# A two-layer attention and feed-forward kernel: three changes where the first feed-forward meets the second attention

## The chip, the cores and the metric

The kernel runs on one core of a Trainium2 chip. The metric is device time in microseconds (us) of one launch, as the median of several runs. Lower is better.

The engines are named as the profile names them: PE is TensorE (PEld its weight loads), DVE is VectorE, ACT is ScalarE, POOL is GpSimd, SP is SyncE, which here only issues DMAs.

## The reference

Two layers, each an attention and a feed-forward, work on `x` of 2 x 1024 tokens by 512. Every part is normed before and after and added to the stream.

```python
x = x + ln(L0_attn(ln(x)))      # per-token attention over groups of heads, no mixing of tokens
x = x + ln(L0_ffn(ln(x)))       # weights rounded to -1, 0, 1; hidden size 1408
x = x + ln(L1_attn(ln(x)))
x = x + ln(L1_ffn(ln(x)))       # silu(gate) * up, 2 of 4 kept; hidden size 2048

def L1_attn(x):                 # 16 heads of 32, 4 key and value heads, causal
    q, k, v = rope(x @ q_w.T), rope(x @ k_w.T), x @ v_w.T
    logits = einsum('bhqd,bhkd->bhqk', q, repeat(k, 4)) / sqrt(32)
    probs = softmax(logits + causal_mask)
    return einsum('bhqk,bhkd->bhqd', probs, repeat(v, 4)) @ c_w.T
```

The change touches the end of `L0_ffn` and all of `L1_attn`.

## The kernel before, in words

**Tiles and groups.** The 2048 tokens are 16 tiles of 128; four tiles make a group of 512 (`GT` = 4, `NG` = 4). `x` stays in SBUF as `x_sb`.

**First feed-forward.** For each group `g` a loop runs over 11 chunks `hc` of the hidden size. A chunk is 16 products into two PSUM banks (`l0_hidden`, L381), a sigmoid on ACT, a product on DVE (L387), a cast on ACT (L389) and a difference on POOL (L390), and later 8 products into four banks `po` (`l0_out`, L400) that stay open for the whole group. The output products trail the chunks through the list `pend`; at chunk 2 none are issued, and the last ones of a group fall into the first two chunks of the next. After the last, DVE and ACT norm the four banks and POOL adds them to `x_sb` (L421).

**The next stage's parts.** During the chunks of the last group the kernel already projects the tiles of batch 0 for the second attention. `project_parts` returns three functions per tile: `first` norms the tile and transposes it (`pxt`, `xT`), `second` makes `pq` and `pkv` (L570, L575) and the rotary products on DVE, whose sums go to POOL (`ra`, L602), and `third` transposes the result (`pkT`, `pqT`), splits it into a high and a low half on ACT and DVE (L617, L618) and writes both halves to DRAM (`dq`, L622, on SP). In the loop they are placed at L809 to L828:

```python
if 1 <= hc <= 2 * GT:
    if hc % 2:
        parts[hc // 2][0]()
        if hc > 1:
            parts[hc // 2 - 1][2]()
    else:
        parts[hc // 2 - 1][1]()
elif hc == 2 * GT + 1:
    parts[GT - 1][2]()
```

After the fourth tile's `third`, at chunk 9, `fill_k` and `fill_q` read keys and queries back from `dq` (L650, L645) into the tile `qk`. At chunk 10 the first scores are interleaved with the last outputs.

**Attention in two passes.** There are 16 tasks: batch, query group `Q`, key head. A first pass makes the scores (`score_step`: `psc`, L665 and the mask L671), takes their maximum on DVE (`mxs`, L676) and sums their exponentials on ACT (L678). The exponentials themselves are thrown away: they go to a tile `junk` in SBUF, and only the sum (`sms`) is used. For task 0 the tile is borrowed from the feed-forward's `h`. From maximum and sum DVE forms one shift per row (`shifts`). A second pass makes the scores again, transposed and shifted (`prob_step`: `pst`, L970 and L977), and ACT's exponential (L983) writes probabilities `pT`; on diagonal blocks POOL zeroes what lies ahead (`affine_select`, L985). `value_step` multiplies by the values one step later (`po`, L999).

**Outputs.** When the four heads of a query group are done, `output_parts` gives one part per tile, run one per step: four products into a bank `py` (L1015), statistics, an inverse root in 13 small DVE instructions (`inverse_root`, L198 to L205), the norm from PSUM into `tmpy` (L209), and an addition to `x_sb` on POOL (L1023), held back by `soon` until the selects of the next step are issued.

**Order.** PE and POOL run in the order in which the program is written; in the stretches that the change touches, DVE, ACT and SP instructions are ordered by the framework's scheduler. The dictionary `due` says which parts run behind which of the 96 steps of the second pass. PSUM has 8 banks: four `a`, three `o`, one `v`; `ring` hands out the `a` and `o` banks in turn.

**Weight pieces.** Sums of the second feed-forward's weights are prepared on POOL (L473) in tiles of 8 blocks of which 7 are used.

Of the kernel before, what the change touches and what calls it, by code (L numbers as in the profile page):

```python
# [9 lines left out]
F32 = mybir.dt.float32  # L10
# [14 lines left out]
def two_layer_sandwich(  # L25
# [406 lines left out]

    def left_piece(pool, tag, bufs, n, i):

        w = pool.tile([P, 8, 2, P], F32, tag=tag, name=f"wl_{n}_{i}", bufs=bufs)
        nc.sync.dma_start(
            out=w[:, 0:4].rearrange("p b c m -> p (b c m)"), in_=(f1_wg, f1_wu)[i][n]
        )
        kept[n, i] = dw.tile([P, 4, 2, P], F32, tag="kept", name=f"kept_{n}_{i}")
        a11, a12, a22, a21, s1_, s2_, s4_ = (w[:, k] for k in range(7))  # L440
        return kept[n, i], w, (
            (s1_, a21, a22, ALU.add), (s2_, s1_, a11, ALU.subtract),
            (a21, a11, a21, ALU.subtract), (s4_, a12, s2_, ALU.subtract),
        )

    def right_piece(pool, tag, bufs, S, j):

        w = pool.tile([P, 8, HW], F32, tag=tag, name=f"wr_{S}_{j}", bufs=bufs)
# [207 lines left out]
    def score_step(tk, q, k, ii, ch, heads, bank, waste):  # L656


        g, i = tk.g, GT * tk.Q + ii
        k0 = ch * GW  # L660
        k1 = min(k0 + GW, (i + 1) * P)
        w = k1 - k0
        for r in heads:
            pa = bank(f"psc_{tk.nm}_{ii}_{ch}_{r}")
            nc.tensor.matmul(  # L665
                pa[:, :w], q.bitcast(F32R)[:, r, ii * P : (ii + 1) * P],
                k.bitcast(F32R)[:, g, :w],
                start=True, stop=True,
            )
# [6 lines left out]
            nc.vector.tensor_reduce(mx, pa[:, :w], AX.X, ALU.max, negate=True)  # L676
            junk = waste(f"junk_{tk.nm}_{ii}_{ch}_{r}")
            nc.scalar.activation(  # L678
                junk[:, :w], pa[:, :w], AF.Exp, bias=mx, accum_out=tk.sm[:, ii, r, ch : ch + 1]
            )  # L680

    with tc.manual_schedule(engines={mybir.EngineType.PE, mybir.EngineType.Pool}):
# [69 lines left out]
        for g in range(NG):  # L752
            nxt = None
            for hc in range(HC):
# [5 lines left out]
                    for c in range(DC):  # L760
                        quant_apply(w3, raw3, th3, c)
                if g == NG - 1 and hc == HC - 1:
                    def waste0(name):
                        return s0.tile([P, GW], F32, tag="h", name=name).bitcast(BF16)

                    tk = tasks[0]
                    score_sums(tk, aw)
                    halves = [
                        lambda ii=ii, r=r: score_step(
                            tk, tk.q, tk.st.k[0], ii, 0, range(r, r + 2), ps_a, waste0  # L770
                        )
                        for ii in range(GT) for r in (0, 2)
                    ]
# [17 lines left out]
                if g + 1 < NG:  # L791
                    if hc == 2:
                        at = l0_softmax(g + 1)
                        ao = l0_values(g + 1, at)
                    if hc == 3:
                        l0_add(g + 1, ao)
                    if hc == 4:
                        nxt = l0_xT_stats(g + 1)
                    if hc in (6, 7):
                        for k in (0, 1):  # L800
                            l0_xT_norm(nxt, 2 * (hc - 6) + k)
                    if hc in (7, 8):
                        ks = (2 * (hc - 7), 2 * (hc - 7) + 1)
                        l0_xT(nxt, ks, [ps_a(f"pt_f{g + 1}_{k}") for k in ks])
                else:

                    if hc == 0:
                        parts = [project_parts(batch(0), i, on_act=i > GT + 1) for i in range(TB)]
                    if 1 <= hc <= 2 * GT:  # L809
                        if hc % 2:  # L810
                            parts[hc // 2][0]()
                            if hc > 1:
                                parts[hc // 2 - 1][2]()
                        else:
                            parts[hc // 2 - 1][1]()
                    elif hc == 2 * GT + 1:
                        parts[GT - 1][2]()
                        done[0] = GT
                        parts[GT][0]()


                        tk = tasks[0]
                        tk.st = batch(0)
                        both = big("qk", F32)[:, : 2 * NKV * GW].rearrange(
                            "p (n r t) -> p n r t", n=2, r=REP
                        )
# [53 lines left out]
    def in_pieces(m, name):  # L880

        nonlocal n_pm
        pm = pms[n_pm % 2]
        n_pm += 1
        r1 = s1.tile([P, GT, REP], F32, tag="r1", name=f"r1_{name}")
        nc.vector.tensor_copy(pm[:, :, :, 0], m)
        nc.vector.tensor_tensor(r1, m, pm[:, :, :, 0], ALU.subtract)
        nc.vector.tensor_copy(pm[:, :, :, 1], r1)
        nc.vector.tensor_tensor(pm[:, :, :, 2], r1, pm[:, :, :, 1], ALU.subtract)
        return pm  # L890
# [52 lines left out]
    def shifts(tk):  # L943

        m, sm = tk.mx[:, :, :, 0], tk.sm[:, :, :, 0]
        if tk.Q > 0:
            n = tk.Q + 1
            m = s1.tile([P, GT, REP], F32, tag="mfin", name=f"mfin_{tk.nm}")
            nc.vector.tensor_reduce(m, tk.mx[:, :, :, :n], AX.X, ALU.min)
            d = s1.tile([P, GT, REP, n], F32, tag="md", name=f"md_{tk.nm}")  # L950
# [57 lines left out]

    def output_parts(st, Q):

        def part(ii):
            nm = f"{st.b}_{Q}_{ii}"
            py = ring(f"py_{nm}")
            for c in range(DC):
                nc.tensor.matmul(  # L1015
                    py, st.oT[Q][:, c, ii * P : (ii + 1) * P], wc1[:, c, :],
                    start=(c == 0), stop=(c == DC - 1),
                )
            mv, rs = ln_stats(s1, [py], f"y_{nm}", roots=False)
            xt = x_sb[:, st.b * TB + GT * Q + ii, :]  # L1020
            tmp = s1.tile([P, D], F32, tag="xn", name=f"tmpy_{nm}", bufs=1)
            ln_apply(tmp, py, mv, rs, 0)
            soon(lambda: nc.gpsimd.tensor_tensor(xt, xt, tmp, ALU.add))  # L1023

        return [lambda ii=ii: part(ii) for ii in range(GT)]

    tw = aw_stack.enter_context(tc.tile_pool(name="tw", bufs=1, side="right"))

# [53 lines left out]
    with tc.manual_schedule(engines={mybir.EngineType.PE, mybir.EngineType.Pool}):  # L1082
# [9 lines left out]
            s_end[tk.n] = n  # L1092
        pos = s_end[0]

        def waste(name):
            return s1.tile([P, GW], BF16, tag="junk", name=name, bufs=3)

        def scored(tk):
            shifts(tk)
            later(first[tk.n] - 1, [lambda: maxima_T(tk)])  # L1100
# [1 line left out]
        def scores_up_to(n, step, between=lambda: None):  # L1102
            nonlocal pos
            while pos < min(n, len(s_steps)):
# [3 lines left out]
                    assert loaded[0] > tk.n  # L1108
                    score_sums(tk, s1)
                for r in (0, 2):  # L1110
                    score_step(tk, tk.q, tk.st.k[ch], ii, ch, range(r, r + 2), ring, waste)
                    if r == 0:
                        between()
                pos += 1
# [544 lines left out]
```

## Time and profile before

| | us |
|---|---|
| median of 3 runs | 1542.98 (1542.07 to 1544.12) |
| the profiled execution's own time | 1541.6 |
| its span, from first to last instruction | 1539.8 |
| PE busy | 1468.4 (95%) |
| DVE busy | 1019.3 (66%) |
| ACT busy | 727.3 (47%) |
| POOL busy | 319.2 (21%) |

The profile is of one execution. Times in it are counted from the start of the span. The last group of the first feed-forward begins near 302 us, the first score of the second attention is at 395.84, its last value product near 928, and the second feed-forward fills the time from about 950 on. In a row of the timeline the numbers are start and duration in us, then engine, line, operation, what is written and what is read; a bracket says how long the engine had been idle and whose end released it.

### The profile page before, as it was taken

Reading aid. Unit: us, or ns where it says so; the run is one execution under the profiler, and the core shown is the slowest. Engines: PE = TensorE matmul, PEld = TensorE weight load, DVE = VectorE, ACT = ScalarE, POOL = GpSimd, SP = SyncE. Lnnn points to the kernel's source line nnn. Section 1 sums busy time; section 2 is a strip of 40 time slices with the busy share of each in tenths; the row PEclk is TensorE's granted clock in tenths of the full one; section 3 lists DMA queues with packets and bytes.
Section 4 is the critical chain, followed back from the end, with each engine's and each line's share of the span. In section 5 each row is a group of like instructions: output and inputs, shape, how many; then the busy total and the mean of one; then the engine's idle time right before and its main releaser. Section 6 shows DMA issues by size and latency. Waiting matters only on the chain.

```text
span 1539.8 us, 20389 instructions
## 1 busy us (share of the span) xinstructions
PE 1468.4 (95%) x6998; PEld 1052.8 (68%) x6998; DVE 1019.3 (66%) x2420; ACT 727.3 (47%) x1847; POOL 319.2 (21%) x424
## 2 busy tenths in 40 slices
PE   7999999999788898999899999999999999999997
PEld 4558887777555454544444446888888888888886
DVE  6976465652477777657777645785578468846783
ACT  4243343332376655798686982451245034404420
POOL 1104475342132313332332011000100020001001
PEclk9999999999899899999899999999999999999998
DMA  7200211201374332343550002643353345235412
GB/s 294 76 14 28 82 55 42 55 18 53 95 178 114 88 102 92 96 141 97 144 158 14 2 1 103 232 144 144 137 212 109 143 171 191 97 143 206 157 48 75
DMA packets 78871, 167.52 MB, mean 109 GB/s; under 512 B 10224, under 2 KB 35824, under 8 KB 76720
## 3 DMA queue, kind: packets, MB, share of 16 engines
q1 hardware_dynamic: 72928, 148.39, 29.8%
q0 software_dynamic: 4784, 16.52, 2.8%
q10 hardware_dynamic: 1056, 1.31, 0.3%
q8 instruction: 55, 0.90, 0.2%
q14 instruction: 48, 0.39, 0.1%
HBM read 138.94 MB, written 27.26 MB: 108 GB/s over the span
## 4 chain that ended last, share of the span: by engine, by line
PE 78%; DVE 10%; ACT 7%; issue 2%; DMA 1%; POOL 1%; SPq 0%; ACTq 0%; DVEq 0%; POOLq 0%
PE acc L1419 13%; PE ph L381 9%; PE pb_u L1268 7%; PE pb_g L1268 7%; ACT junk L678 4%; PE po L400 4%; PE psc L665 4%; PE pq L258 4%; PE pc_u L1268 4%; PE pc_g L1268 4%; PE py L1015 4%; PE pst L970 3%; PE po L999 3%; PE pq L570 3%; DVE mxs L676 3%; ACT pT L983 2%
## 5 line engine op out<-in xcount | busy, mean ns | idle before, releaser
L676 DVE TENSOR_REDUCE mxs<-psc 128x1 f32<-128x512 f32 (+3 forms) x384 | 195.6, 550 | 88.9 <-PE psc L671 47.0
L678 ACT ACTIVATE junk<-psc,mxs 128x512 bf16<-128x512 f32 (+3 forms) x384 | 222.2, 631 | 32.3 <-DVE mxs L676 28.2
L983 ACT ACTIVATE pT<-pst 128x512 f32<-128x512 f32 (+3 forms) x384 | 160.4, 554 | 91.1 <-PE pst L977 90.7
L381 PE MATMUL ph<-xTg,w 128*128 128x512 f32 x704 | 172.3, 398 | 1.7 <-DVE xTg L371 0.9
L381 PEld LDWEIGHTS ph<-xTg,w 128*128 128x128 f32 x704 | 132.3, 189 | 31.6 <-DVE xTg L371 1.2
L1472 POOL TENSOR_TENSOR x_sb<-x_sb,o 128x512 f32<-128x512 f32 x14 | 19.1, 1364 | 549.4 <-DVE o L209 549.2
L1419 PE MATMUL acc<-wd,h 128*128 128x256 f32 x512 | 121.6, 379 | 0.0
L1419 PEld LDWEIGHTS acc<-wd,h 128*128 128x128 f32 x512 | 97.0, 190 | 13.1
L985 POOL TENSOR_SCALAR_AFFINE_SELECT pT<-pT 128x256 f32<-128x256 f32 x128 | 52.1, 415 | 253.2 <-ACT pT L983 251.2
L665 PE MATMUL psc<-k,q 128*128 128x512 f32 (+3 forms) x256 | 92.3, 429 | 6.4 <-ACT junk L678 5.3
L678 ACT ACTIVATION_READ_ACCUMULATOR junk<-psc,mxs 128x1 f32 x384 | 98.0, 256 | 0.0
L970 PE MATMUL pst<-q,k 128*128 128x512 f32 (+3 forms) x256 | 80.0, 405 | 14.7 <-ACT junk L678 9.7
L999 PE MATMUL po<-pT,v 128*32 128x512 f32 (+3 forms) x768 | 92.6, 521 | 1.3 <-POOL pT L985 0.9
L1419 PE MATMUL acc<-wd,hx 128*128 128x256 f32 x384 | 93.3, 379 | 0.0
L400 PE MATMUL po<-w,hl 128*128 128x512 f32 x352 | 89.9, 398 | 0.4 <-DVE tmp L209 0.3
L390 POOL TENSOR_TENSOR hl<-h,hl 128x512 fp32r<-128x512 f32 x44 | 57.3, 1307 | 158.0 <-ACT hl L389 157.9
L387 DVE TENSOR_TENSOR h<-h,ph 128x512 f32<-128x512 f32 x44 | 30.0, 684 | 80.1 <-PE ph L381 70.0
L665 PEld LDWEIGHTS psc<-k,q 128*128 128x128 f32 x256 | 49.4, 202 | 46.9 <-ACT pT L983 20.9
L1419 PEld LDWEIGHTS acc<-wd,hx 128*128 128x128 f32 x384 | 73.0, 190 | 9.9
L1329 DVE TENSOR_TENSOR gate<-gate,ab 128x1024 f32<-128x1024 f32 x32 | 39.2, 1225 | 59.2 <-ACT ab L1326 59.2
L400 PEld LDWEIGHTS po<-w,hl 128*128 128x128 f32 x352 | 66.8, 191 | 15.8 <-DVE tmp L209 1.3
L970 PEld LDWEIGHTS pst<-q,k 128*128 128x128 f32 x256 | 45.0, 197 | 47.7 <-ACT junk L678 23.9
(287 smaller groups left out, 2983.6 us busy)
## 6 DMA issues: line engine op xcount, KB each, us to landing
w<-kept SPq DMA_DIRECT2D x64, 512.0 KB, 5.9
wd<-keptd SPq DMA_DIRECT2D x16, 1024.0 KB, 8.7
q<-dq SPq DMA_DIRECT2D x60, 256.0 KB, 4.8
w<-in_f_wg SPq DMA_DIRECT2D x32, 384.0 KB, 3.4
w<-in_f_wu SPq DMA_DIRECT2D x32, 384.0 KB, 5.4
wd<-in_f_wd SPq DMA_DIRECT2D x16, 768.0 KB, 6.7
dq<-hl SPq DMA_DIRECT2D x32, 320.0 KB, 3.2
kept<-wl POOLq DMA_DIRECT2D x16, 512.0 KB, 3.0
```

The source lines that it names most:

```text
L258: nc.tensor.matmul(pa[:, :n], xT[:, c, :], w[:, c, :], start=(c == 0), stop=False)
L381: nc.tensor.matmul(pa, wt[:, c, cols], xT[:, s, c, :], start=(c == 0 and s == 0), stop=(c == DC - 1 and s == 1),)
L400: nc.tensor.matmul(pos0[g][k], hl[:, s, k * P : (k + 1) * P], w3[:, hc, :], start=(hc == 0 and s == 0), stop=(hc == HC - 1 and s == 1),)
L665: nc.tensor.matmul(pa[:, :w], q.bitcast(F32R)[:, r, ii * P : (ii + 1) * P], k.bitcast(F32R)[:, g, :w], start=True, stop=True,)
L676: nc.vector.tensor_reduce(mx, pa[:, :w], AX.X, ALU.max, negate=True)
L678: nc.scalar.activation(junk[:, :w], pa[:, :w], AF.Exp, bias=mx, accum_out=tk.sm[:, ii, r, ch : ch + 1])
L970: nc.tensor.matmul(pas[r][:, c0:], st.k[j // GT].bitcast(F32R)[:, g, (j % GT) * P : (j % GT + 1) * P], tk.q.bitcast(F32R)[:, r, c0:], star ...
L983: nc.scalar.activation(p[:, e, c0:], pas[2 * pr + e][:, c0:], AF.Exp)
L999: nc.tensor.matmul(tk.po[DK * r : DK * r + DK, c0:], st.v[j // GT][:, j % GT, g * DK : (g + 1) * DK], tk.pT[j, r // 2][:, r % 2, c0:], sta ...
L1015: nc.tensor.matmul(py, st.oT[Q][:, c, ii * P : (ii + 1) * P], wc1[:, c, :], start=(c == 0), stop=(c == DC - 1),)
L1268: nc.tensor.matmul(p, a[:, c, :], b[:, c, :], start=(first and c == 0), stop=(c == 1), skip_group_check=not first,)
L1419: nc.tensor.matmul(acc[m // 2][:, m % 2 * HW : (m % 2 + 1) * HW], a[:, j, k * P : (k + 1) * P], b[:, j, :], start=start, stop=True, skip_g ...
```

## The change

Three things are done.

1. The parts of tiles 0 to 3 start at chunk 0 of the last group instead of chunk 1, and with them everything up to `fill_k` and `fill_q`, which move from chunk 9 to chunk 8. Chunk 9 then has no part.
2. In the first pass the exponential writes over its own scores in PSUM; the `junk` tiles go.
3. The output norms of a group of four tiles are made together: each part copies its bank `py` to SBUF and takes statistics from there; a fifth part, one step later, forms the four inverse roots in one set of 13 instructions, norms the four tiles in place and hands four additions to POOL. The very last query group of the last batch keeps single norms from PSUM.

Beside these, some tiles get smaller or single: 7 blocks instead of 8 for the weight pieces, one buffer for `r1` and `md`. The four output tiles take the place of `xn` and three new tiles `y1` to `y3`.

```diff
-        w = pool.tile([P, 8, 2, P], F32, tag=tag, name=f"wl_{n}_{i}", bufs=bufs)
+        w = pool.tile([P, 7, 2, P], F32, tag=tag, name=f"wl_{n}_{i}", bufs=bufs)
...
             nc.vector.tensor_reduce(mx, pa[:, :w], AX.X, ALU.max, negate=True)
-            junk = waste(f"junk_{tk.nm}_{ii}_{ch}_{r}")
             nc.scalar.activation(
-                junk[:, :w], pa[:, :w], AF.Exp, bias=mx, accum_out=tk.sm[:, ii, r, ch : ch + 1]
+                pa[:, :w], pa[:, :w], AF.Exp, bias=mx, accum_out=tk.sm[:, ii, r, ch : ch + 1]
             )
...
-                    if 1 <= hc <= 2 * GT:
-                        if hc % 2:
+                    if hc < 2 * GT:
+                        if hc % 2 == 0:
                             parts[hc // 2][0]()
-                            if hc > 1:
+                            if hc > 0:
                                 parts[hc // 2 - 1][2]()
                         else:
-                            parts[hc // 2 - 1][1]()
-                    elif hc == 2 * GT + 1:
+                            parts[hc // 2][1]()
+                    elif hc == 2 * GT:
                         parts[GT - 1][2]()
                         done[0] = GT
                         parts[GT][0]()
...
-        r1 = s1.tile([P, GT, REP], F32, tag="r1", name=f"r1_{name}")
+        r1 = s1.tile([P, GT, REP], F32, tag="r1", name=f"r1_{name}", bufs=1)
...
     def output_parts(st, Q):
+        nm = f"y_{st.b}_{Q}"
+        alone = st.b == B - 1 and Q == NQ - 1
+        n = 1 if alone else GT
+        ys = {}
+
+        def y_of(ii):
+            tag = "xn" if alone or ii == 0 else f"y{ii}"
+            return s1.tile([P, D], F32, tag=tag, name=f"tmp{nm}_{ii}", bufs=1)
+
+        def add(tiles, mv, ys):
+            rs = inverse_root(s1, mv, n, f"{nm}_{tiles[0]}")
+            for k, ii in enumerate(tiles):
+                ln_apply(ys[ii], py_of.pop(ii) if alone else ys[ii], mv, rs, k)
+                xt = x_sb[:, st.b * TB + GT * Q + ii, :]
+                soon(lambda xt=xt, y=ys[ii]: nc.gpsimd.tensor_tensor(xt, xt, y, ALU.add))
+
+        py_of, got = {}, []
+
         def part(ii):
-            nm = f"{st.b}_{Q}_{ii}"
-            py = ring(f"py_{nm}")
+            py = py_of[ii] = ring(f"p{nm}_{ii}")
             for c in range(DC):
                 nc.tensor.matmul(
                     py, st.oT[Q][:, c, ii * P : (ii + 1) * P], wc1[:, c, :],
                     start=(c == 0), stop=(c == DC - 1),
                 )
-            mv, rs = ln_stats(s1, [py], f"y_{nm}", roots=False)
-            xt = x_sb[:, st.b * TB + GT * Q + ii, :]
-            tmp = s1.tile([P, D], F32, tag="xn", name=f"tmpy_{nm}", bufs=1)
-            ln_apply(tmp, py, mv, rs, 0)
-            soon(lambda: nc.gpsimd.tensor_tensor(xt, xt, tmp, ALU.add))
-
-        return [lambda ii=ii: part(ii) for ii in range(GT)]
+            ys[ii] = y_of(ii)
...
+            stats, mv = got
+            k = 0 if alone else ii
+            if not alone:
+                nc.vector.tensor_copy(ys[ii], py)
+            nc.vector.bn_stats(out=stats[:, k, :], in_=py if alone else ys[ii])
+            nc.vector.bn_aggr(out=mv[:, k, :], in_=stats[:, k, :])
+            if alone:
+                add([ii], mv, ys)
+
+        parts = [lambda ii=ii: part(ii) for ii in range(GT)]
+        return parts if alone else parts + [lambda: add(list(range(GT)), got[1], ys)]
```

More of the change, by code (lines that the diff above doesn't have):

```diff
@@ L446, in right_piece @@
     def right_piece(pool, tag, bufs, S, j):
-        w = pool.tile([P, 8, HW], F32, tag=tag, name=f"wr_{S}_{j}", bufs=bufs)
+        w = pool.tile([P, 7, HW], F32, tag=tag, name=f"wr_{S}_{j}", bufs=bufs)
         nc.sync.dma_start(
@@ L654, in score_sums, with score_step @@
         tk.sm = pool.tile([P, GT, REP, NQ], F32, tag="sms", name=f"sms_{tk.nm}", bufs=3)
-    def score_step(tk, q, k, ii, ch, heads, bank, waste):
+    def score_step(tk, q, k, ii, ch, heads, bank):
         g, i = tk.g, GT * tk.Q + ii
@@ L762, in two_layer_sandwich @@
                 if g == NG - 1 and hc == HC - 1:
-                    def waste0(name):
-                        return s0.tile([P, GW], F32, tag="h", name=name).bitcast(BF16)
                     tk = tasks[0]
@@ L769, in two_layer_sandwich @@
                         lambda ii=ii, r=r: score_step(
-                            tk, tk.q, tk.st.k[0], ii, 0, range(r, r + 2), ps_a, waste0
+                            tk, tk.q, tk.st.k[0], ii, 0, range(r, r + 2), ps_a
                         )
@@ L949, in shifts @@
             nc.vector.tensor_reduce(m, tk.mx[:, :, :, :n], AX.X, ALU.min)
-            d = s1.tile([P, GT, REP, n], F32, tag="md", name=f"md_{tk.nm}")
+            d = s1.tile([P, GT, REP, n], F32, tag="md", name=f"md_{tk.nm}", bufs=1)
             nc.vector.tensor_tensor(
@@ L1018, in part @@
                 )
-            mv, rs = ln_stats(s1, [py], f"y_{nm}", roots=False)
-            xt = x_sb[:, st.b * TB + GT * Q + ii, :]
-            tmp = s1.tile([P, D], F32, tag="xn", name=f"tmpy_{nm}", bufs=1)
-            ln_apply(tmp, py, mv, rs, 0)
-            soon(lambda: nc.gpsimd.tensor_tensor(xt, xt, tmp, ALU.add))
-        return [lambda ii=ii: part(ii) for ii in range(GT)]
+            ys[ii] = y_of(ii)
+            if not got or alone:
+                got[:] = [
+                    s1.tile([P, n, 6], F32, tag=f"st_y{n}", name=f"st_{nm}_{ii}", bufs=1),
+                    s1.tile([P, n, 2], F32, tag=f"mv_y{n}", name=f"mv_{nm}_{ii}", bufs=2),
+                ]
+            stats, mv = got
[8 more added lines that the diff above has]
+        return parts if alone else parts + [lambda: add(list(range(GT)), got[1], ys)]
     tw = aw_stack.enter_context(tc.tile_pool(name="tw", bufs=1, side="right"))
@@ L1093, in two_layer_sandwich @@
         pos = s_end[0]
-        def waste(name):
-            return s1.tile([P, GW], BF16, tag="junk", name=name, bufs=3)
         def scored(tk):
@@ L1110, in scores_up_to @@
                 for r in (0, 2):
-                    score_step(tk, tk.q, tk.st.k[ch], ii, ch, range(r, r + 2), ring, waste)
+                    score_step(tk, tk.q, tk.st.k[ch], ii, ch, range(r, r + 2), ring)
                     if r == 0:
```

## The prediction, made before the changed kernel ran

> **What bounds the kernel now.** I read the page first (engine shares, then the slices), then busy time by stretch, then TensorE's own waits in the attention stage, then the timeline around each wait of over 2 us.
>
> ```profile
> PE 1468.4 (95%) x6998; PEld 1052.8 (68%) x6998; DVE 1019.3 (66%) x2420; ACT 727.3 (47%) x1847; POOL 319.2 (21%) x424
> ...
> L678 ACT ACTIVATE junk<-psc,mxs 128x512 bf16<-128x512 f32 (+3 forms) x384 | 222.2, 631 | 32.3 <-DVE mxs L676 28.2
> ```
>
> TensorE is busy 95% of the span; only its idle time, or time at a lower clock, can be won. The stretches say where that is: the second feed-forward after 960 us shows none until its tail and is not touched. It lies in the last group of the first feed-forward (300 to 400) and in attention (400 to 960). Columns: stretch, length, then busy us (instructions) of PE, PEld, DVE, ACT, POOL, granted clock, DMA share, GB/s.
>
> ```profile
> 300.00:400.00 100.00, 94.13 (x400) 71.93 (x399) 36.06 (x94) 26.63 (x54) 29.02 (x26) 0.97 0.20 48
> 400.00:960.00 560.00, 520.40 (x2754) 275.39 (x2753) 382.36 (x1183) 395.25 (x1206) 151.92 (x253) 0.94 0.33 92
> ```
>
> In attention TensorE idles 39.6 us and runs part of the rest slowly. Its waits there (engine, line, releaser: us in all, times, longest), and four short stretches of TensorE alone (stretch, length, PE busy, clock, DMA share, GB/s):
>
> ```profile
> PE pst L970 <- ACT junk L678: 12.8, 42, 1.0
> PE psc L665 <- ACT junk L678: 10.2, 13, 2.9
> PE pst L970 <- DVE tmpy L209: 4.0, 1, 4.0
> PE psc L665 <- DVE rbk L598: 3.4, 1, 3.4
> ```
>
> ```profile
> 390.60:395.80 5.20, 0.15 (x1) 0.89 0.79 151
> 395.80:405.20 9.40, 8.58 (x27) 0.51 0.01 3
> ...
> 589.00:593.00 4.00, 0.00 (x1) 0.96 0.29 82
> 593.10:599.80 6.70, 6.70 (x28) 0.52 0.17 49
> ```
>
> The reader is to see two holes, 5.2 us at 390.6 and 4.0 us at 589, and that behind each TensorE runs at half its clock for 9.4 and 6.7 us. A hole is paid twice: idle alone is 9 us for the two, with what the slow stretches cost about 14 (worked out below).
>
> ```profile
> 318.20 0.81 DVE L209 TENSOR_SCALAR tmp<-po,mv_f0o,rs_f0o 128x512 f32<-128x512 f32 x1 [0.67 <-POOL x_sb L421]
> ...
> 379.04 0.60 PE L490 MATMUL pqT<-ident,ra 128*128 128x128 f32 x4
> 383.67 1.77 SPq L650 DMA_DIRECT2D qk<-dq  x4
> 395.84 0.45 PE L665 MATMUL psc<-qk 128*128 128x128 f32 x1 [5.09 <-DMA qk<-dq]
> ...
> 592.17 0.81 DVE L209 TENSOR_SCALAR tmpy<-py,mv_y,rs_y 128x512 f32<-128x512 f32 x1
> 593.03 1.01 PE L970 MATMUL pst<-q,k 128*128 128x256 f32 x3 [4.03 <-DVE tmpy L209]
> ```
>
> The first hole is a round trip through DRAM: from the last transposes of the fourth tile (pqT, ending 379.6) to the first score (395.84) pass 16.2 us. The second is a PSUM bank: the fourth `py` is held from its last product (585.8) until the norm has read it (593.0). The row at 318.20 is one of the four norms at the change of group, each behind a POOL addition.
>
> **Part 1: parts one chunk earlier.** Nothing is added; TensorE's list holds the same 5653 instructions. The four tiles' three parts, their ACT copies (0.59, 0.27, 0.27, 0.60), DVE products, POOL sums (0.46 and 1.28 per tile) and SyncE's eight writes and eight reads of `dq` move one chunk up. On SP they pass nothing but each other; on POOL each tile's sums now stand ahead of the `hl` difference (1.3) of the chunk that they pass. ACT (27 of 100 us) and DVE (36 of 100) have room.
>
> End of the stage: behind the last transposes TensorE now has pxt 0.4, ph 3.5, po 1.8, ph 3.6, pq and pkv 5.2, po 1.8 = 16.4 us (durations of 380 to 391 us), against the round trip's 16.2. The 5.1 us hole closes. Of the 9.4 slow us I keep only part: the third and fourth scores still need DVE's maximum, a table load (1.28) and the first exponential, so the way from the first score to `pq` shrinks from 7.5 to about 5.5, and `pq` from 4.24 to 3.44: 2.8 us. What is late next is TensorE's wait at 429.77 (3.43, on DVE's products), which follows the end of this feed-forward and shifts with it.
>
> Start of the stage, the loss: `pq`, `pkv` of tile 0 now come straight after the previous group's last `po`, before the chunk, and the transposes of tile 0 one chunk later. By the built order DVE does the previous group's four norms between the products of tile 0. From the rows of 307 to 324 us, shifted: TensorE wants pxt of tile 1 at 322.3. DVE's `pq` product ends 317.7; the norms, each waiting for a POOL addition (1.27; the row at 318.20), end about 322.5; the rest of the products 323.5; `xn` 324.1. POOL's fourth addition ends 324.2 and tile 0's two sums 326.0, and the transposes of tile 0 need them. So TensorE idles about 1.8 and 1.4 us: +3.3 us with hand-offs. Bounds: +2 (the products slip ahead of the norms) to +6.5 (half-clock follows, 3.4 us windows costing 1.7 each). I take 3.3.
>
> Part 1: -5.1 - 2.8 + 3.3 = -4.6.
>
> **Part 2: exponentials in place in PSUM.** 384 ACT instructions write their input bank instead of SBUF; a `junk` buffer goes. No row has ACT writing PSUM. Nearest rows: the 512-wide exponentials to SBUF as bf16 here repeat every 0.66 us with the 0.19 sum read, those of `pT` as fp32 every 0.52 without it, so the written type costs nothing. [...] The bank's release stays at the sum read. [...] No reason excludes a loss: reading and writing one bank at once might cost up to the streaming time again (rival 2). I take -1.5, nearer the row. That task 0 no longer borrows the feed-forward's `h` buffers costs and gives nothing: TensorE's waits there are on PSUM.
>
> **Part 3: norms in fours.** For three of four output groups (the last keeps its single norms) DVE's rows (duration ns least/median/most):
>
> ```profile
> L203 DVE TENSOR_TENSOR nv_y<-rs_y x48: 142/159/1191, 561.1 to 947.7; 128x1 f32<-128x1 f32 x48
> L209 DVE TENSOR_SCALAR tmpy<-py,mv_y,rs_y x16: 776/810/812, 565.2 to 948.4; 128x512 f32<-128x512 f32 x16
> L209 DVE TENSOR_SCALAR xnf<-x_sb,mv_f,rs_f x20: 533/544/3154, 93.0 to 916.9; 128x512 f32<-128x512 f32 x20
> ```
>
> Away: 9 inverse roots of 13 small instructions, 117 x 0.155 = 18.1; 12 norms from PSUM at 0.81 = 9.7. Added: 12 copies from PSUM at 0.68 (as `oT` at L1007) = 8.2, 12 norms from SBUF at 0.544 = 6.5. Net -13.1 us of DVE's 382. Only what TensorE waited for counts: `py` is now held for a copy (0.68) instead of 4 us, so the 4.0 hole closes, and of the slow 6.7 us I take 2.0, since ACT (1.2 us wait at 596.9) would hold the rest anyway. The group at 721 to 748 had only 1.6 us of waits on ACT: -0.5. The one at 808 to 833 none.
>
> Against it: four additions of 1.27 reach POOL in one block of 5.1 us, past two selects of the step and one weight sum, and ahead of the next step's selects (the built order puts them before the last diagonal step, or before the fourth of task (1,0,1)). The values that need those selects come a step (5 to 7 us) later, so cover is nearly whole; without it, 1 to 2 us in each place. [...] Since POOL's block is held until the next step's selects, I take one stop a group and, for two groups, 0.5 us of it reaching TensorE: +1.0 (none for the group at 808, where TensorE waits for nothing).
>
> Part 3: -4.0 - 2.0 - 0.5 + 1.0 = -5.5. Smaller pieces (7 blocks for 8) and single buffers: no instruction moves, 0; `r1` and `md` belong to DVE's own order.
>
> **Sum.** -4.6 - 1.5 - 5.5 = -11.6 against the profiled execution's 1541.6 (span 1539.8 and 1.8 around it): 1530.0. The median shown, 1542.98, is 1.4 above that execution: 1531.4.
>
> **Rivals.** (1) The holes only move: the start of the group idles over 3.4 us and goes to half clock (+6.5), POOL's blocks cost 1.5 at each of two places, ACT gives nothing. -5.1 - 2.8 + 6.5 - 6.0 + 3 + 1 = about -3: 1540, and up to 1547 if a further slow window of 3.4 to 6.8 us falls elsewhere. For: the clock is at half in 12 windows between 395 and 960 us now, several after holes of under 3 us (465, 531). Against: the holes at the earlier group changes (190 to 195) brought none.
> (2) Slower: an exponential in place costs more. Of 384 about a third, 128, lie before a wait of TensorE; the gain of 10 us without part 2 is gone at +0.08 us each. If reading and writing the bank alternate, a mean width of 320 at 0.83 ns adds 0.27: 128 x 0.27 = 34 us, 1543 - 10 + 34 = 1567, ACT then busy 500 of 560. For: no row shows it. [...]
> [...]
>
> **How the numbers follow.** The sum 0.60 (1525 to 1539), rival 1 0.20 (a quarter faster, over half same), rival 2 0.13, rival 3 0.07. About 0.2%, 3.1 us, is what a measurement can tell: faster is below 1539.9, same up to 1546.1. Faster 0.60 + 0.05 + 0.07 = 0.72, same 0.12, slower 0.03 + 0.13 = 0.16. The range, 1522 to 1546, leaves out rival 2 and the tails.
>
> **What would show it.** Right: the first score starts near 394 with under 1 us of DMA wait and a clock near 1.0; a hole of 2 to 4 us near 323; no wait of `pst` on a norm near 590; L678 at or below 631 ns mean; DVE some 13 us less. Wrong: L678 above 0.7 us, a slow clock at 323 to 330, `po` waiting on POOL's selects, or the feed-forward's end not earlier.

## The result, and the profile after

The changed kernel takes 1548.85 us (median of 9 runs, 1544.92 to 1551.4) against 1542.98 of the kernel before in the same comparison: a ratio of 1.0039 with a 95% interval from 1.0025 to 1.0052. By that ratio it is 6.0 us slower, where 11.6 us less were forecast. The profiled execution after took 1547.8 us (span 1546.1). In the page of the kernel after, these are the lines that answer to the two shown of before:

```profile
PE 1469.6 (95%) x6998; PEld 1053.5 (68%) x6998; DVE 1016.3 (66%) x2315; ACT 726.5 (47%) x1847; POOL 320.7 (21%) x424
...
L677 ACT ACTIVATE psc<-psc,mxs 128x512 f32<-128x512 f32 (+3 forms) x384 | 217.7, 605 | 45.8 <-DVE mxs L676 44.7
```

The exponentials (L677 now) are 26 ns shorter, and yet ACT waits 44.7 us for DVE's maxima ahead of them where it waited 28.2. DVE has 105 instructions fewer and only 3.0 us less to do, not 13. Busy time by stretch (columns as in the prediction), then TensorE's largest waits from 290 to 970 us:

```profile
300.00:400.00 100.00, 95.98 (x409) 72.46 (x408) 37.31 (x95) 27.41 (x57) 27.99 (x26) 0.98 0.20 48
400.00:960.00 560.00, 513.53 (x2712) 269.97 (x2711) 377.54 (x1075) 389.99 (x1195) 153.75 (x253) 0.92 0.32 88
```

```profile
PE psc L665 <- ACT psc L677: 17.1, 13, 7.0
PE pst L966 <- ACT psc L677: 15.5, 44, 3.9
PE psc L665 <- DVE rbk L598: 3.4, 1, 3.4
```

The same two waits in the kernel before, from 290 to 970 us:

```profile
PE pst L970 <- ACT junk L678: 12.8, 42, 1.0
PE psc L665 <- ACT junk L678: 11.0, 14, 2.9
```

The first feed-forward's end is better: TensorE is busy 1.85 us more of those 100. In the 560 us of attention it is busy 6.87 us less, and its clock falls from 0.94 to 0.92. The two waits that were to go, on the DMA of `qk` and on a norm, are not in the list any more; the two waits on ACT's sums have grown from 23.8 to 32.6 us, and their longest from 2.9 to 7.0. Stretches of the kernel after, for TensorE alone (stretch, length, PE busy, clock, DMA share, GB/s):

```profile
323.10:325.20 2.10, 1.52 (x8) 0.61 0.00 0
393.50:403.50 10.00, 8.55 (x40) 1.00 0.01 2
589.00:593.00 4.00, 2.59 (x21) 1.00 0.33 91
593.00:600.00 7.00, 6.31 (x27) 1.00 0.17 44
750.50:757.50 7.00, 0.00 (x0) 0.73 0.00 0
757.50:767.00 9.50, 8.47 (x34) 0.50 0.53 122
840.00:844.00 4.00, 0.11 (x2) 0.80 0.00 0
844.00:852.50 8.50, 8.08 (x33) 0.50 0.01 2
```

Rows 2 to 4 are the two places of the forecast: the first scores run at full clock, and of the 4.0 us near 590 are 1.4 left, at full clock. The last four are new: 7.0 and 3.9 us without a matmul at two places where TensorE waited 1.0 us or less before, each with 8.5 to 9.5 us at half clock behind it. The timeline of the kernel after at the first of them:

```profile
750.94 0.17 DVE L932 SCALAR_TENSOR_TENSOR lgp<-lgp,lgy 128x16 f32<-128x16 f32 x1
751.02 0.54 DVE L209 TENSOR_SCALAR tmpy<-tmpy,mv_y,rs_y 128x512 f32<-128x512 f32 x1
751.11 6.05 POOL L1022 TENSOR_TENSOR x_sb<-x_sb,tmpy 128x512 f32<-128x512 f32 x4 [0.88 <-DVE lgp L932]
751.48 1.28 DVE L933 SCALAR_TENSOR_TENSOR lgp<-lgp,lgy 128x16 f32<-128x16 f32 x1
752.68 0.54 DVE L209 TENSOR_SCALAR tmpy<-tmpy,mv_y,rs_y 128x512 f32<-128x512 f32 x1
753.13 1.23 DVE L934 SCALAR_TENSOR_TENSOR lgp<-lgp,lgz 128x16 f32<-128x16 f32 x1
...
754.74 1.23 DVE L935 SCALAR_TENSOR_TENSOR lgw<-lgp,lgw 128x16 f32<-128x16 f32 x1
755.90 0.68 DVE L676 TENSOR_REDUCE mxs<-psc 128x1 f32<-128x512 f32 x1
...
756.67 0.66 ACT L677 ACTIVATE psc<-psc,mxs 128x512 f32<-128x512 f32 x1 [6.95 <-DVE mxs L676]
757.50 0.47 PE L665 MATMUL psc<-k,q 128*128 128x128 f32 x1 [7.04 <-ACT psc L677]
```

Read it from the bottom: TensorE waits 7.04 us for a bank that an exponential on ACT holds; ACT waits 6.95 us for a maximum on DVE; that maximum stands in DVE's queue behind the four norms and the end of the logarithm's chain (the small steps, L920 to L936, that turn the sums into part of the shifts). And those crawl: steps of 128x16 that take 0.17 at 750.94 take 1.23 to 1.28 while POOL has its four additions, which take 1.5 each.

A third loss shows no hole. Followed matmul for matmul, the kernel after is 6.0 us ahead of the kernel before at 440 us (times of the kernel before) and 1.1 behind at 520. The place near 590 brings it 5.4 ahead at 600; it is 7.0 ahead at 754, level at 758 past the first new hole, 5 to 6 behind at 842 to 850 past the second, and 6.2 behind at the end of attention. The stretch of the same 467 matmuls, before and then after:

```profile
440.00:530.00 90.00, 81.15 (x467) 0.94 0.49 124
```

```profile
434.00:530.90 96.90, 87.07 (x467) 0.84 0.46 115
```

TensorE's waits there add up to 7.1 and 8.0 us. So some 6 of the 6.9 us are clock: three periods at half clock in the first row, nine in the second. It is no mark of part 2 by itself: against the trace of before, those of e5 and e10 below, with exponentials to SBUF, lose 2.6 and 5.6 us from 440 to 520 as well. How often the clock falls has to be read from many executions.

### The profile page after: what moved, and what is told of

It reads as the page before. It is cut to its first block, busy times and chain, and to the rows that moved or that the text cites. A ratio compares the mean times of both kernels' runs of the same rounds, so it can differ in the third digit from the quotient of the medians.

```text
span 1546.1 us, 20266 instructions
## 1 busy us (share of the span) xinstructions
PE 1469.6 (95%) x6998; PEld 1053.5 (68%) x6998; DVE 1016.3 (66%) x2315; ACT 726.5 (47%) x1847; POOL 320.7 (21%) x424
## 3 DMA queue, kind: packets, MB, share of 16 engines
q1 hardware_dynamic: 72928, 148.39, 29.7%
## 4 chain that ended last, share of the span: by engine, by line
PE 78%; DVE 11%; ACT 7%; issue 2%; POOL 1%; DMA 0%; ACTq 0%; DVEq 0%; SPq 0%; POOLq 0%
PE acc L1440 12%; PE ph L381 9%; PE pb_u L1289 7%; PE pb_g L1289 7%; ACT psc L677 4%; PE po L400 4%; PE py L1029 4%; PE pq L258 4%; PE pst L966 4%; PE pc_u L1289 4%; PE pc_g L1289 4%; PE psc L665 4%; PE po L995 3%; PE pq L570 3%; DVE mxs L676 3%; ACT pT L979 2%
## 5 line engine op out<-in xcount | busy, mean ns | idle before, releaser
L676 DVE TENSOR_REDUCE mxs<-psc 128x1 f32<-128x512 f32 (+3 forms) x384 | 194.3, 550 | 88.0 <-PE psc L671 44.7
L677 ACT ACTIVATE psc<-psc,mxs 128x512 f32<-128x512 f32 (+3 forms) x384 | 217.7, 605 | 45.8 <-DVE mxs L676 44.7
L1440 PEld LDWEIGHTS acc<-wd,h 128*128 128x128 f32 x512 | 97.0, 190 | 13.1
L677 ACT ACTIVATION_READ_ACCUMULATOR psc<-psc,mxs 128x1 f32 x384 | 98.2, 256 | 0.0
L665 PEld LDWEIGHTS psc<-k,q 128*128 128x128 f32 x256 | 49.7, 204 | 53.0 <-ACT psc L677 16.2
L966 PEld LDWEIGHTS pst<-q,k 128*128 128x128 f32 x256 | 46.6, 204 | 45.1 <-ACT psc L677 25.3
L400 PEld LDWEIGHTS po<-w,hl 128*128 128x128 f32 x352 | 65.7, 188 | 15.5 <-DVE tmp L209 1.3
```

Source lines behind the costliest of these rows:

```text
L400: nc.tensor.matmul(pos0[g][k], hl[:, s, k * P : (k + 1) * P], w3[:, hc, :], start=(hc == 0 and s == 0), stop=(hc == HC - 1 and s == 1),)
L665: nc.tensor.matmul(pa[:, :w], q.bitcast(F32R)[:, r, ii * P : (ii + 1) * P], k.bitcast(F32R)[:, g, :w], start=True, stop=True,)
L677: nc.scalar.activation(pa[:, :w], pa[:, :w], AF.Exp, bias=mx, accum_out=tk.sm[:, ii, r, ch : ch + 1])
L966: nc.tensor.matmul(pas[r][:, c0:], st.k[j // GT].bitcast(F32R)[:, g, (j % GT) * P : (j % GT + 1) * P], tk.q.bitcast(F32R)[:, r, c0:], star ...
L1440: nc.tensor.matmul(acc[m // 2][:, m % 2 * HW : (m % 2 + 1) * HW], a[:, j, k * P : (k + 1) * P], b[:, j, :], start=start, stop=True, skip_g ...
```

## The experiments

All are ratios to the kernel before, run in turn with it on one chip; 0.1% is 1.54 us. The runs fall into several comparisons, on different chips, each with its own runs of the kernel before, so kernels are set against each other by their ratios and not by their medians. The last column is worked out from each execution's span and mean granted clock: 2 x (1 - clock) x span / 3.413, averaged, the number of 3.41 us periods at half clock (in the traces of before and after, the half-clock stretches of attention are one to four times 3.413 us long). The kernel before has 26.6 to 27.7 of them in the four comparisons of e1 to e15.

| kernel | median us | ratio, 95% interval | periods |
|---|---|---|---|
| after (parts 1, 2, 3) | 1548.85 | 1.0039 [1.0025, 1.0052] | 29.4 |
| e1, parts 1 and 2 | 1544.68 | 1.0015 [1.0004, 1.0025] | 28.5 |
| e2, after, norms and additions spread | 1545.87 | 1.0018 [1.0008, 1.0028] | 31.2 |
| e3, after, without 12 additions | 1541.44 | 0.9997 [0.9984, 1.0009] | 26.6 |
| e4, after, 12 norms on ACT | 1543.46 | 1.0008 [0.9999, 1.0017] | 26.7 |
| e5, part 1 | 1537.60 | 0.9969 [0.9958, 0.9980] | 23.3 |
| e6, part 2 | 1546.89 | 1.0024 [1.0017, 1.0032] | 29.7 |
| e7, parts 2 and 3 | 1551.75 | 1.0056 [1.0038, 1.0073] | 31.6 |
| e8, e1 with 46 filling matmuls | 1552.05 | 1.0051 [1.0036, 1.0066] | 25.3 |
| e9, in-place exponentials only | 1546.67 | 1.0031 [1.0020, 1.0042] | 30.8 |
| e10, the rest of part 2 only | 1541.18 | 0.9992 [0.9980, 1.0003] | 26.9 |
| e11, part 1 with 27 filling matmuls | 1535.71 | 0.9958 [0.9943, 0.9973] | 20.3 |
| e12, before, order fixed | 1553.84 | 1.0080 [1.0066, 1.0094] | 30.0 |
| e13, e12 and exponentials in place | 1556.07 | 1.0098 [1.0083, 1.0113] | 33.7 |
| e14, part 1 and early release | 1543.12 | 1.0008 [0.9999, 1.0017] | 25.0 |
| e15, e14 with the 27 fillers | 1540.63 | 0.9990 [0.9979, 1.0002] | 20.1 |

**What part 3 costs (e1 to e4).** e1 has `output_parts` of before in the kernel after. 

> The changed kernel with the attention outputs normed tile by tile as before (parts 1 and 2 kept, part 3 undone). Theory A (part 3 is what costs: four POOL additions beside DVE work that reads and writes SBUF, with the score maxima queued behind it): TensorE's holes of 7.0 us at 757 and 3.9 us at 844 go, the stall near 593 comes back; of the 10.0 us that the changed kernel loses against the kernel before between 701 and 881 (from 3.7 ahead to 6.3 behind) nothing is left: 1540 to 1545 us. Theory B (the exponentials in place are what costs): still slow, about 1549 or more. Theory C (the parts one chunk earlier cost, through the hole at 323 and a colder clock after it): 1547 to 1551.

1544.68. Part 3 costs 0.24% (3.7 us) on top of parts 1 and 2, which fits A; but parts 1 and 2 together are not the -6.1 us of the forecast, they are +2.3. So part 3 is not all of it. In e2 the fifth to eighth parts take one norm and one addition each:

```diff
-        return parts if alone else parts + [lambda: add(list(range(GT)), got[1], ys)]
+        return parts if alone else parts + [lambda ii=ii: add([ii], got[1], ys) for ii in range(GT)]
```

(the root is made once, in the first of them). 

> The changed kernel, the inverse root still for four tiles at once, but one norm with its addition in each of the fifth to eighth parts in place of four in the fifth. Theory A: with one addition (about 1.3 us) for each step there is no longer a row of POOL additions for DVE to run into; at most one DVE instruction for each addition is stretched; the holes at 757 and 844 go and the stall at 593 stays away: 1535 to 1541 us. Theory B or C: as slow as the changed kernel, 1546 to 1551.

1545.87, inside neither range: better than the kernel after, no better than e1. The hole at 757 is 2.2 us and the one at 844 is gone, but one of 2.3 us has come at 608, and half clock is more frequent than in any kernel with parts 1 and 2. e3 drops the additions:

```diff
-                soon(lambda xt=xt, y=ys[ii]: nc.gpsimd.tensor_tensor(xt, xt, y, ALU.add))
+                if alone:
+                    soon(lambda xt=xt, y=ys[ii]: nc.gpsimd.tensor_tensor(xt, xt, y, ALU.add))
```

> The changed kernel with POOL's additions of the normed attention outputs left out for three of the four groups (12 additions; the residual sum lacks these outputs): the four norms stay in a row on DVE. Theory A: without POOL beside them the four norms take 2.1 us, no DVE operation of the logarithm's chain is over 0.4 us, the holes at 757 and 844 are under 1.5 us, 1535 to 1541 us. Theory D (the row of four norms and thirteen small instructions ahead of the maxima is itself what costs, whatever POOL does): the holes stay at two thirds of their size or more, 1544 to 1549 us.

1541.44, 0.42% below the kernel after and just above A's range. In the timeline of e3 the same stretch of DVE:

```profile
755.70 0.54 DVE L209 TENSOR_SCALAR tmpy<-tmpy,mv_y,rs_y 128x512 f32<-128x512 f32 x1
756.16 0.17 DVE L933 SCALAR_TENSOR_TENSOR lgp<-lgp,lgy 128x16 f32<-128x16 f32 x1
756.25 0.54 DVE L209 TENSOR_SCALAR tmpy<-tmpy,mv_y,rs_y 128x512 f32<-128x512 f32 x1
756.70 0.17 DVE L934 SCALAR_TENSOR_TENSOR lgp<-lgp,lgz 128x16 f32<-128x16 f32 x1
```

Every step has its short time again: L933 0.17 instead of 1.28. The addition on POOL is what stretched it. But the holes are not under 1.5 us as A wanted. TensorE's waits from 740 to 850 us, in the kernel after, in e3 and in e1:

```profile
PE psc L665 <- ACT psc L677: 8.2, 3, 7.0
PE pst L966 <- ACT psc L677: 7.3, 12, 3.9
```

```profile
PE psc L665 <- ACT psc L677: 5.6, 4, 4.3
PE pst L966 <- ACT psc L677: 4.9, 11, 2.0
```

```profile
PE pst L966 <- ACT psc L677: 5.7, 13, 1.0
PE psc L665 <- ACT psc L677: 0.9, 2, 0.5
```

These waits add up to 6.6 us without the fours (e1), 10.5 with the row alone (four norms and the steps of the root, e3), 15.5 with the additions beside it (after). So D has its share: 3.9 us of waits are the row itself ahead of the maxima, 5.0 the collision. e4 moves the norms to ACT:

```diff
-                ln_apply(ys[ii], py_of.pop(ii) if alone else ys[ii], mv, rs, k)
...
+                    nc.scalar.activation(
+                        ys[ii], ys[ii], AF.Identity, scale=rs[:, k : k + 1], bias=mv[:, k, 0:1]
+                    )
```

(for all but the last group; the mean's column then holds minus mean times root). 

> The changed kernel with the four norms on ACT (Identity with scale and bias) for three of the four groups; POOL's four additions stay. Theory A: the maxima no longer stand behind norms that are stopped; what DVE has left in SBUF beside the additions (the logarithm's chain at 750, small operations) may still be stretched, up to four times 1.2 us in the second group; ACT has 4 times about 0.6 us more to do ahead of its exponentials, 2.4 us for each group: 1538 to 1545 us. Theory D: the row is only moved to ACT, in front of the exponentials, 1543 to 1549 us.

1543.46, inside both ranges: it does not tell A from D, and its holes (3.9 and 3.1 us) say that a row ahead of the exponentials is little better than one ahead of the maxima.

**Parts one by one (e5 to e7).** 

> The kernel before with part 1 alone (next stage's parts one chunk earlier). Theory E (the 3 to 5 us that part 1 wins by 409 us of the span are won, and are lost again between 440 and 535, where TensorE's granted clock is halved for a few periods more than before): 1541 to 1545 us, no more than 0.1% from before, the half-clock stretches at about 446, 487 and 514 as in the run without the fours. Theory F (part 1 wins what was forecast, -4.6, and the exponentials in place are what took it back): 1536 to 1539 us.

1537.60, ratio 0.9969: -4.8 us, in F's range: part 1 by itself brings what was forecast, and keeps it.

> The kernel before with part 2 alone (exponentials in place in PSUM, with the buffers that this frees). Theory E: -1.5 us or nothing, 1540 to 1543 us. Theory F: slower than before by 3 us or more, 1545 to 1549 us, although each exponential is some 26 ns shorter on ACT.

1546.89, +3.7 us: part 2 alone is a loss, again F.

> Parts 2 and 3 without part 1 (the parts from the second chunk on, as before). Theory A with the size that the run without the fours gave (part 3 costs about 4 us): 1544 to 1548 us, the hole at about 757 to 761 over 5 us again. If part 3's price hangs on where part 1 has put the work: within 0.1% of before, 1541 to 1544 us.

1551.75, above both ranges; the hole at 755.8 is 7.05 us. Part 3 on top of part 2 costs 0.32%, so its price does not come from where part 1 has put the work. From before: part 1 -4.8, then part 2 +7.1 (e5 to e1), then part 3 +3.7. The parts don't add: part 2 costs 3.7 us alone and 7.1 beside part 1; why is not shown.

**What in part 2 costs (e9, e10, e12, e13).** e9 changes the destination alone, e10 the rest.

```diff
-            junk = waste(f"junk_{tk.nm}_{ii}_{ch}_{r}")
...
-                junk[:, :w], pa[:, :w], AF.Exp, bias=mx, accum_out=tk.sm[:, ii, r, ch : ch + 1]
+                pa[:, :w], pa[:, :w], AF.Exp, bias=mx, accum_out=tk.sm[:, ii, r, ch : ch + 1]
```

> The kernel before with the exponentials in place alone: every buffer keeps its size (weight tiles of 8 blocks, two buffers for the two small tiles). Theory G (part 2 costs its 4 us because the exponentials' own 26 ns shift the work of 440 to 535 us against the clock's periods, with no wait added): 1545 to 1548 us, 29 to 31 periods at half clock on average. Theory H (the smaller buffers of the logarithm's chain and of the weights cost it): 1540.5 to 1543 us, 27 periods as before.

> The kernel before with the rest of part 2 alone: weight tiles of 7 blocks, one buffer in place of two for two small tiles; the exponentials go to SBUF as before. Theory G: 1541 to 1543.5 us, as before. Theory H: 1545 to 1548 us.

1546.67 and 1541.18, both as theory G has it: it is the exponentials. But ACT is no slower. Three lines of ACT's timeline, of the kernel before and then of e9:

```profile
645.22 0.69 ACT L678 ACTIVATE junk<-psc,mxs 128x512 bf16<-128x512 f32 x1
645.81 0.19 ACT L678 ACTIVATION_READ_ACCUMULATOR junk<-psc,mxs 128x1 f32 x1
645.90 0.68 ACT L678 ACTIVATE junk<-psc,mxs 128x512 bf16<-128x512 f32 x1
```

```profile
649.20 0.66 ACT L677 ACTIVATE psc<-psc,mxs 128x512 f32<-128x512 f32 x1
649.78 0.19 ACT L677 ACTIVATION_READ_ACCUMULATOR psc<-psc,mxs 128x1 f32 x1
649.88 0.65 ACT L677 ACTIVATE psc<-psc,mxs 128x512 f32<-128x512 f32 x1
```

The exponential is 0.03 shorter, and the next one starts 0.68 after it in both: its end lies under the sum's read. Over the 512-wide ones that follow each other within 1 us (133 and 131 of them) the median from start to start is 663 ns in both. So nothing was won, and TensorE's longest waits in attention are the same in both traces (2.9, 3.4 and 4.0 us). Two things did change: the scheduler gave ACT, DVE and SP another order at the start of attention (between 415 and 455 us: two casts behind two exponentials of `pT`, maxima ahead of `hl` differences, query reads ahead of `dq` writes), and there is more half clock, 30.8 periods against 27.7. In e12 and e13 the order of these three engines is written out from the prologue to attention's fourth step, and is the same in both; in the two traces the instructions of each engine stand in one order from 281 to 957 us. 

> The kernel before, with the order of DVE, ACT and SP from the scores' prologue to attention's fourth step as written in the code in place of the scheduler's. Not meant to be faster: it is the partner of the next run. 1540 to 1556 us.

> The same with the exponentials in place in PSUM; every engine's order is then that of its partner. Theory I (writing the exponentials to PSUM costs nothing, the 3 to 5 us of part 2 are those of the changed order at 415 to 450 us): within 1.5 us of its partner. Theory G (the destination itself does it): 3 to 6 us slower than its partner.

1553.84 (1551.90 to 1555.45, 6 runs) and 1556.07 (1555.28 to 1558.06, 4 runs): 2.2 us apart, between the two theories; the intervals of the ratios overlap, so that there is a cost with one order is likely rather than shown. In the traces e13's matmuls of attention start 0.0 to 1.1 us ahead of their partners up to 859 us, and 1.9 to 3.3 behind them after 900. What differs comes later, in TensorE's rows of e12 and then of e13 (stretch, length, PE busy, clock, DMA share, GB/s):

```profile
400.00:850.00 450.00, 404.84 (x2112) 0.92 0.40 108
850.00:912.00 62.00, 57.53 (x326) 0.97 0.00 1
```

```profile
400.00:850.00 450.00, 404.49 (x2113) 0.92 0.40 108
850.00:912.00 62.00, 57.94 (x306) 0.89 0.01 1
```

Much the same holes (4.5 and 4.1 us without a matmul), another clock: 0.97 and 0.89 from 850 to 912 us, and 20 matmuls fewer done in that time. With one order, in-place writing shows as half-clock periods (33.7 against 30.0 on average), not as a wait. Why it has more of them is open: the order is excluded here, and TensorE's mean busy share in the periods that a half clock followed is 0.55 in both kinds of kernel.

**What half clock follows from, and its price (e8, e11, e14, e15).** Cut into periods of 3.41 us by the edges of its half-clock stretches, attention from 395 to 910 us, in the ten traces with exponentials in place and the seven without, shows this: of 1,822 periods at full clock in which TensorE was busy over 0.82 of the time, one was followed by half clock; of 313 below 0.80, 209 were. Below 0.44 all 60 were; between 0.76 and 0.80 it was 56 of 82, but between 0.72 and 0.76 only 6 of 38, so the share alone does not decide; what does beside it is not shown. e8 fills holes with matmuls of zero weights:

```diff
+        for i in range(n):
+            nc.tensor.matmul(
+                po.rearrange("p (n t) -> p n t", n=4), zerob,
+                onesb.unsqueeze(1).to_broadcast([P, 4, P]),
+                start=first, stop=True, skip_group_check=not first,
+            )
```

> The run without the fours (parts 1 and 2), with 46 bf16 matmuls of a zero weight tile put in TensorE's queue into five holes (5, 12, 9, 7 and 13 of them, about 0.2 us each, ahead of the instruction that waits; they write an unused bank, or add zeros to the open sum of the values). Nothing that is waited for comes sooner. Theory E: without the idle period no half clock follows at about 425, 463, 535 and 596; of the 97 us at half clock some 25 to 35 go, and with 0.3 to 0.5 us each 8 to 15 us of time: 1530 to 1538 us. If the half clock only goes with the holes and costs nothing by itself, or if the fillers delay what comes behind them: 1543 to 1549 us.

1552.05, a miss (the 18 executions reach from 1538.8 to 1554.1, and the trace is of one of 1547.5): the first filler, ahead of `pq`, needs a bank that DVE still reads for the feed-forward's norms, and TensorE stood 5.4 us for it; behind the one near 590 a hole of 2.6 us came at 598. Periods did go, 28.5 in e1 to 25.3. e11 has part 1 alone, and fillers only where no bank is waited for. 

> Part 1 alone, with 27 bf16 matmuls of a zero weight tile in three of TensorE's holes (10 at 424, 10 at 460, 7 at 529, about 0.23 us each); the filler that waited 5.4 us for a bank, and the one in the hole near 590, are left away. Theory E (a period at half clock costs about 1.5 us, and follows from a hole): of the 23.3 periods of part 1 alone 4 to 6 go, 1529 to 1533 us. If it is only correlated: 1537 to 1540 us.

1535.71, between its two ranges: 3.0 periods fewer than e5 and 0.11% less time (the intervals overlap). TensorE from 440 to 490 us, in e5 and then in e11:

```profile
440.00:490.00 50.00, 43.91 (x246) 0.87 0.55 130
```

```profile
440.00:490.00 50.00, 47.29 (x273) 0.97 0.59 148
```

The clock there rises from 0.87 to 0.97. e11 has the lowest ratio of this study, 0.42% below the kernel before. e14 asks whether the hole near 590 can be ended without the row:

```diff
-            mv, rs = ln_stats(s1, [py], f"y_{nm}", roots=False)
...
-            ln_apply(tmp, py, mv, rs, 0)
+            nc.vector.tensor_copy(tmp, py)
+            mv, rs = ln_stats(s1, [tmp], f"y_{nm}", roots=False)
+            ln_apply(tmp, tmp, mv, rs, 0)
```

> Part 1 alone, and each attention output copied from PSUM to SBUF (16 DVE copies of about 0.69 us more) and normed there tile by tile, with its addition in its own step: the bank comes free before the statistics, with no row of four norms and no row of four additions. The 4.0 us of TensorE near 590 go, at most one DVE instruction runs into each addition: 1532 to 1536 us. If DVE's 8 to 9 us more come onto the path: 1538 to 1543 us.

> The run before this one with the 27 filling matmuls in the three holes at 424, 460 and 529 as well: what both bring adds up, 1529 to 1534 us; if the period grid takes one of them back, as fast as part 1 with the filled holes alone, 1534 to 1537 us.

1543.12 and 1540.63: e14 is at the upper end of its second case, and e15 above both of its ranges. In e14's trace the wait of 4.0 us on the norm is gone, but two others stand there, 1.4 us on the copy and 2.2 on `xT`, and half clock follows: its matmuls are 3.2 us ahead of e5's before the place and 3.2 ahead behind it, at 598. They are 3.9 behind at 877, after new holes of 1.0 to 1.8 us at 752, 832 and 836 and more half clock behind them. e15 against e14 repeats the fillers' effect: 4.9 periods and 0.18% fewer.

What does a period cost? The two pairs with fillers give about 0.6 us for each that is taken away, with overlapping intervals. The stretch from 440 to 530 us gave some 6 us for six. And the 149 executions of the kernel before, in their four comparisons, differ among themselves: a straight line through time against periods rises by 0.8 to 1.0 us per period. That last is a correlation, but by it the 3.1 periods that e9 has more than before answer for 2.5 to 3 of its 4.8 us; where the rest comes from is not shown.

## Why the prediction was wrong, point by point

The forecast was -4.6, -1.5 and -5.5 for the three parts; one after the other they measured -4.8, +7.1 and +3.7. Two steps failed: in part 2, that exponentials in place would bring TensorE 1.5 us and change nothing else; in part 3, the +1.0 for what the batch of four does to DVE's queue.

- **Part 1, -4.6: right.** Alone it is -4.8 us (e5). The hole for the DMA is gone and the first score starts at 393.55, as the timeline of the kernel after shows:

```profile
393.55 0.22 PE L665 MATMUL psc<-qk 128*128 128x128 f32 x1
...
396.06 0.33 PE L665 MATMUL psc<-qk 128*128 128x128 f32 x1 [1.45 <-ACT psc L677]
```

  The half clock behind it is gone (393.5 to 403.5 at 1.00). The cover was a close thing: the terms set against the round trip's 16.2 us add up to 16.3, not 16.4. The loss at the start, put at +3.3, was 2.0 of idle ahead of 323.13, 0.5 ahead of 324.58 and one period at half clock. That slow clock was named as a sign of being wrong; it came, and part 1 held all the same. The stall that was at 429.77 came at 424.20.
- **Part 2, -1.5: the sign was wrong.** No run shows that term. The instruction got 26 ns shorter (605 for 631), but a row of them goes on at the 0.66 us of the nearest row, since the sum's read (0.19) covers its end: 0 would have been right for this term. What came instead is a loss of 3.7 us alone and 7.1 beside part 1, without a new wait, in more periods at half clock (29.7 against 27.3 alone). Rival 2 had the sign for another reason: exponentials that cost more. They don't. The prediction expected no other order of DVE, ACT and SP from this part, and put no price on a changed clock. Why the clock is lower stays open.
- **Part 3, -5.5: it is +3.7 (after against e1) or +4.9 (e7 against e6).** The gain was there in its place: no `pst` wait on a norm near 590, full clock behind it. The +1.0 against it was the term that failed, in two ways. One was the stops: the sum has one a group (a DVE step held up beside a POOL addition), with 0.5 us of it reaching TensorE, and no run shows that term. From 750.48 to the first maximum at 755.90 the four norms and the chain's last steps took 5.4 us, against 2.2 in e3, and there the steps that were stopped are three of the chain, 1.23 to 1.28 us for 0.17; at 839 to 842 they are two norms, 1.5 us each for 0.54. That the additions wait for the next step's selects did not part them: they began at 751.11, while the second norm ran. The other was not in the sum: even without POOL the row of four stands ahead of the maxima, 3.9 us of TensorE's waits from 740 to 850. "None for the group at 808, where TensorE waits for nothing" was wrong too: DVE's delay arrived as a wait of 3.9 us at 840.
- **DVE -13.1 us: 3.0.** In e3, with 12 fewer additions on POOL, it is 1010.5, 8.8 below before; the stretched steps of the kernel after took back 5.8 of these. The other 4.3 were not there to save: the small steps of the roots overlap with their neighbours (the 208 instructions of the roots in the kernel before add up to 34.1 us and fill 24.1 that nothing else on DVE fills), so a sum of their durations counts time twice.
- **The clock.** Rival 1 said that holes only move and named the half-clock windows; the new holes are not at the change of group, where it put them, but at POOL's two later blocks, where it had 1.5 each. It also allowed for one more slow stretch of 3.4 to 6.8 us elsewhere; from 440 to 530 us there were six periods more, 20.5 us at half clock, and that is the largest single loss in the trace.

## What to carry to other kernels

Ahead of a batch of small steps ask what stands behind it in the same queue: the batches of four left DVE 3.0 us less to do and yet delayed the score maxima, then the exponentials, then the banks. Where DVE works in SBUF beside a block of POOL instructions, as here where steps of 0.17 us took 1.23 to 1.28, price every stop in full unless something in the built order keeps them apart. With TensorE at 95%, judge an edit by what it leaves of idle time in one place: here half clock followed 56 of the 82 periods with 0.7 to 0.8 us of idle in 3.41, and six more periods at half clock came with some 6 us lost from 440 to 530 us, where the waits had grown by only 0.9.

## What the runs showed of the hardware that was not expected

- A DVE step of 128x16 went from 0.17 to 1.23 us beside POOL's additions, and these from 1.27 to 1.5; with the additions left out the step is back at 0.17.
- Half clock came after periods with TensorE busy up to about 0.8 (56 of the 82 between 0.76 and 0.80), not only after an idle one; over 0.82 it came once in 1,822.
- The 149 executions of the kernel before differ by 0.8 to 1.0 us for each period of 3.41 us at half clock that they have more.
- Writing an exponential to PSUM shortened the instruction by 26 ns and left the pace of a row of them at 0.66 us; with every engine's order the same, 33.7 periods at half clock stood against 30.0.
